# Pacing of expert tiles between attention turns: round length, a floor on the rest, and one exemption

## Chip, cores and metric

One core of one Trainium2 chip. The metric is the device time of one execution in microseconds (us); the kernel before takes 1529.41 us in the median of three executions (1528.07 to 1531.95).

## The reference

One transformer layer on x of shape (16, 512, 128), float32: attention with 16 heads of 8 and a residual, layernorm, then a mixture of 8 experts, of which each token uses two, a residual, layernorm.

```python
probs = softmax(Q @ K.T / sqrt(8)); iv = probs with key 0 set to 0, renormalised
x = layernorm(x + (0.5 * probs + 0.5 * iv) @ V @ Wo.T + bo)
wte = routing weights of the two chosen experts (0 for the other six)
out = sum over e of wte[:, e] * ((silu(x @ w1[e].T) * (x @ w3[e].T)) @ w2[e].T)
x = layernorm(x + out)
```

## The kernel before

**Turns.** The 16 sequences are worked on one after another, each in 32 turns (UNITS, line 998), 512 turns in all, numbered on from 0. A turn of attention (lines 1076 to 1088) has, on TensorE: two matmuls that spread the negated row maxima over a pair of PSUM banks (L451), two score matmuls for the maxima of 21 turns later (L399), two score matmuls (L456) and, in odd turns alone, the eight products of weights and values (L476). ScalarE takes the exponential of 128x1024 scores (L467). VectorE reduces 128x1024 scores to maxima (L405 to L408; the helper at L126 records it). In the trace a turn begins with its pair of L451 matmuls: there are 1024 of these rows, two for each turn.

**Small steps.** Everything else of the layer is written as generators which yield what they need (a bank: ONE, a pair: PAIR, a pause: REST, and so on). `everything()` (line 1055) hands out steps after each turn's attention. These small steps are projections, values, transposes after attention, routing, and the bank step of the maxima (`put_maxima`, line 410): four small transposes whose result goes by DMA to the tile `mt`, which the L451 matmuls of a later turn read.

**Rounds and tiles.** Tokens are scattered by expert into DRAM (L714, GpSimd) and worked on in tiles of 128 tokens of one expert, 149 tiles in all. Sequences form groups of 7, 7 and 2; each group has rounds, which become ready as attention moves on: of 9, 8, 8, 8, 8 and 22 tiles in a group of 7, and 23 in the last group. One tile takes 13 TensorE operations, called expert operations below: a transpose of the tokens (L133 with `xs`), eight matmuls up (L111 with `yx`, `ws`) and four down (L111 with `ws`, `hT`). Around them are a tanh (L858), a product on VectorE, a copy (L869), a product on GpSimd (L870), a copy of the down result and the transposed tokens to SBUF (L904), an indirect scatter (L912, GpSimd), and two loads that SyncE issues, of 64.5 KB of tokens (L824) and 768 KB of weights (L839). `down_and_turn` (line 877) takes one bank by `one()`: while experts run it is the single bank ELSE, shared with the small steps, and it comes free when ScalarE's copy at L904 has read it.

**The pace.** `experts(rnd)` (line 842) is a generator too. `running` holds the running rounds, two at most; only the first is advanced (line 1160), while the second merely issues its first loads. Work is counted in `dealt` by moving columns, two for each: 256 for an expert matmul, 128 for a transpose, 680 for an even attention turn and 1704 for an odd one. The pace of a turn is set at lines 1148 to 1176:

```python
goal = gen.left / max(gen.until - turn, 1)   # L1150, in the attention turns
goal += BASE                                 # L1155, BASE = 1450
carry += goal
while running and dealt[0] - before_turn < carry: ...one more step of running[0]...
carry = max(-600, min(1200, carry - dealt[0] + before_turn))
```

`left` is what the round still has to deal. `until` (line 1020) is the turn by which it should be through: the next round's earliest turn plus CHAIN (60) plus FILL (12). If the expert step asks for a bank and a small step has taken it in this turn, the expert step is put off and `owed` (line 1163) keeps small bank steps out of the next turn (lines 1116, 1117).

**After the last turn** the remaining tiles are worked on with no attention beside them (about 45 of the 149); here this is called the tail.

Of the kernel before, what the change touches and what calls it, by code (L numbers as in the profile page):

```python
# [33 lines left out]
def post_ln_layer(  # L34
# [375 lines left out]
    def put_maxima(b, half):  # L410

        yield NOW
        nm = nms.pop((b, half)).rearrange("p t s j -> p t j s")
        pc = small.tile([P, NT, 4, NPC, 2], BF16, tag="pc", name=f"pc{b}_{half}")
        for r in range(NPC):
            dve.tensor_copy(pc[:, :, :, r, :], nm)
            if r == 1:
                yield NOW
            if r < NPC - 1:
                rest = small.tile([P, NT, 4, 2], F32, tag="rest", name=f"rest{b}_{half}_{r}")  # L420
                dve.tensor_tensor(rest, nm, pc[:, :, :, r, :], ALU.subtract)
                nm = rest
        yield ONE
        n = 8 * NPC
        pm = one(BF16)
        for t in range(NT):
            turned(
                pm[0:n, t * P : (t + 1) * P],
                pc[:, t, :, :, :].rearrange("p j r s -> p (j r s)"), ident_b,
            )  # L430
        mT = work.tile([n, L], BF16, tag="mT", name=f"mT{b}_{half}", bufs=1)
        nc.scalar.copy(mT, pm[0:n, 0:L])
        mt = operands(b, half)[2]
        for j in range(4):
            nc.sync.dma_start(
                mt[HR * j : HR * j + NPC, :, :], mT[2 * NPC * j : 2 * NPC * (j + 1), :]
            )
# [565 lines left out]
    TOKENS = 4  # L1003
    PAUSE = 2400
    CHAIN = 60
    FILL = 12
    BASE = 1450
    TILE = 12 * 2 * P + P
    READY = [sum(GROUPS[:g]) + n for g, size in enumerate(GROUPS) for n in rounds_of(size)]
# [2 lines left out]
    class Steps:  # L1012
# [4 lines left out]
        def of(self, rnd):  # L1017
            self.rnd, self.left = rnd, rnd.tiles * TILE
            after = [n for n in READY if n > rnd.grp.first + rnd.n]
            self.until = UNITS * min(after, default=B) + CHAIN + FILL  # L1020
            return self
# [33 lines left out]
    def everything():  # L1055
        for gen in (project(0),):
            gen = Steps(gen)
# [4 lines left out]
        turn, last_final, carry, served = -LEAD, -UNITS, 0, dve.walked  # L1062
        before_turn, owed = dealt[0], False
        end = UNITS * B
        while turn < end + 2 or active or running or finishing or ready or late:
# [18 lines left out]
            if ahead:  # L1084
                reduce_maxima(*pm)
                if (turn + LEAD) % 16 == 15:
                    gen = put_maxima((turn + LEAD) // UNITS, (turn + LEAD) % UNITS // 16)
# [14 lines left out]
            if ready and all(gen.rnd.last for gen in running) and len(running) < 2:  # L1102
# [6 lines left out]
            gen = next((  # L1109
                gen for gen in active if gen.need == ONE  # L1110
                or gen.need == LONG and (not busy or gen.last is None or turn - gen.last > 1)
            ), None)

            if owed:
                gen = None
            taken = gen is not None and now
            order = [gen] if gen else []
# [27 lines left out]
                    gen.more()  # L1147
            if running:
                gen = running[0]
                goal = gen.left / max(gen.until - turn, 1)  # L1150
                if turn >= end:
                    goal = TILE // 2
                    spare[0] = 1 if gen.rnd.grp.g < len(GROUPS) - 1 or finishing else 0
                elif turn < end:
                    goal += BASE  # L1155
                carry += goal
            else:
                carry = 0
            while running and dealt[0] - before_turn < carry:
                gen, at = running[0], dealt[0]  # L1160
                if gen.need == TURN:
                    break
                owed = gen.need == ONE and taken
# [14 lines left out]
    with tc.manual_schedule(  # L1178
        engines={
            mybir.EngineType.PE, mybir.EngineType.DVE, mybir.EngineType.Activation,  # L1180
            mybir.EngineType.Pool, mybir.EngineType.SP,
        }
    ):
        everything()
# [37 lines left out]
```

## Time and profile before

| what | value |
|---|---|
| median of three executions | 1529.41 us |
| the profiled execution's own time, its span | 1559.23 us, 1557.5 us |
| turns 0 to 122, before the first expert operation | 49.3 to 338.4 us |
| turns 123 to 510 | 338.4 to 1359.5 us |
| last turn and tail | 1359.5 to 1557.5 us |
| L467 exponential, one | 1023 ns, x512 |
| maxima reduction on VectorE, one | 1220 ns, x512 |
| pair of passes of one expert matmul (L111), each pass | 285 ns, overlapping, x2384 and x1192 passes |

A row of the page's fifth part gives a group of instructions, its busy time, the mean of one in ns, and the idle time before it with what ended that. A float32 matmul has two passes on TensorE, so that its rows count double: four down matmuls are a row "x8". A window row gives, for a stretch of the span, its length, each engine's busy time with the number of instructions, and the granted TensorE clock as a share of full speed.

### The profile page before, as it was taken

How to read it: one execution, taken by the hardware profiler on the slowest of the kernel's cores; microseconds unless marked ns; L12 is line 12 of the kernel's file. 1: busy time of each engine (PE TensorE's matmuls, PEld its weight loads, DVE VectorE, ACT ScalarE, POOL GpSimd, SP SyncE). 2: the span in 40 equal slices, each digit the busy share in tenths (PEclk: the TensorE clock that was granted, in tenths of full speed). 3: DMA queues.
4: the chain of work that ended last, by engine and by line, in shares of the span. 5: the costliest groups of instructions: out<-in, count | busy, mean ns of one | idle time of the engine just before them, and what ended most of it. 6: DMA issues, size and time to landing. Idle time of an engine off the chain costs nothing.

```text
span 1557.5 us, 28295 instructions
## 1 busy us (share of the span) xinstructions
PE 1345.3 (86%) x9933; PEld 766.7 (49%) x9933; DVE 1062.4 (68%) x2221; ACT 890.8 (57%) x1383; POOL 674.6 (43%) x982
## 2 busy tenths in 40 slices
PE   4788888879889899999989999988898899997983
PEld 1222323225455555555555555555554555587883
DVE  5656576767876677767766776777777776465675
ACT  1355555555665666666656666666666677742333
POOL 2001031303534363626355463837364674756443
PEclk6577687868998999989999999999998999998996
DMA  5131443124443535363445366463633443576894
GB/s 187 50 92 65 130 126 118 56 83 172 164 138 129 196 131 193 115 212 129 136 172 173 143 209 209 140 214 110 216 127 104 172 161 126 204 246 230 304 344 155
DMA packets 114781, 248.43 MB, mean 160 GB/s; under 512 B 15232, under 2 KB 47104, under 8 KB 114640
## 3 DMA queue, kind: packets, MB, share of 16 engines
q1 hardware_dynamic: 95024, 220.01, 41.3%
q0 software_dynamic: 8864, 18.24, 3.4%
q10 hardware_dynamic: 10752, 8.39, 1.6%
q8 instruction: 78, 1.28, 0.3%
q14 instruction: 63, 0.52, 0.1%
HBM read 184.04 MB, written 68.04 MB: 162 GB/s over the span
## 4 chain that ended last, share of the span: by engine, by line
PE 56%; DVE 22%; ACT 10%; issue 5%; DMA 4%; POOL 2%; another core or an unknown queue 1%; SPq 1%; ACTq 0%; POOLq 0%; DVEq 0%
PE banks L111 23%; PE banks L476 14%; DVE nm L126 11%; PE banks L451 7%; PE banks L399 6%; ACT ex L467 6%; PE banks L133 4%; PE banks L456 2%; DVE lo L126 1%; ACT hi L339 1%; DMA z<-x1d 1%; DVE pc L126 1%; DVE th L126 1%; DVE z L126 1%
## 5 line engine op out<-in xcount | busy, mean ns | idle before, releaser
L126 DVE TENSOR_REDUCE nm<-banks 128x2 f32<-128x1024 f32 x512 | 623.4, 1220 | 320.9 <-PE banks L399 240.1
L467 ACT ACTIVATE ex<-banks 128x1024 f32<-128x1024 f32 x512 | 524.0, 1023 | 290.7 <-PE banks L456 241.1
L399 PE MATMUL banks<-kt,qt 32*128 32x512 f32 x1024 | 280.0, 548 | 78.6 <-DVE nm L126 57.8
L111 PE MATMUL banks<-yx,ws 128*128 128x128 f32 x2384 | 337.2, 285 | 7.2 <-DVE th L126 2.3
L111 PEld LDWEIGHTS banks<-yx,ws 128*128 128x128 f32 x2384 | 300.9, 197 | 63.3 <-issue 48.7
L476 PE MATMUL banks<-ex,vaug 128*32 128x512 f32 x2048 | 314.4, 690 | 0.0
L456 PE MATMUL banks<-qt,kt 32*128 32x512 f32 x1024 | 313.1, 605 | 0.0
L870 POOL TENSOR_TENSOR hT<-hT,th 128x512 f32<-128x512 f32 x104 | 132.6, 1275 | 337.7 <-ACT hT L869 249.8
L451 PE MATMUL banks<-mt,ones_b 3*128 3x512 bf16 x1024 | 216.3, 415 | 49.5 <-ACT ex L467 34.8
L912 POOL DMA_INDIRECT yd<-yx,toi x149 | 151.9, 1020 | 78.3 <-issue 35.3
L111 PE MATMUL banks<-ws,hT 128*128 128x128 f32 x1192 | 171.3, 289 | 4.3 <-ACT yx L904 2.7
L111 PEld LDWEIGHTS banks<-ws,hT 128*128 128x128 f32 x1192 | 157.3, 205 | 35.4 <-issue 27.6
L399 PEld LDWEIGHTS banks<-kt,qt 32*128 32x128 f32 x1024 | 103.0, 200 | 130.1 <-DVE nm L126 99.3
L451 PEld LDWEIGHTS <-ones_b 3*128 3x128 bf16 x1024 | 59.0, 93 | 193.4 <-issue 148.6
L714 POOL DMA_INDIRECT xg<-x,sloti x128 | 129.7, 1014 | 36.3 <-issue 25.9
L904 ACT COPY yx<-banks 128x128 f32<-128x128 f32 (+1 forms) x201 | 63.4, 316 | 131.5 <-PE banks L111 100.2
L858 ACT ACTIVATE th<-banks 128x512 f32<-128x512 f32 x149 | 88.9, 596 | 78.0 <-PE banks L111 56.2
L126 DVE SCALAR_TENSOR_TENSOR th<-th,banks 128x512 f32<-128x512 f32 x149 | 101.2, 679 | 46.4 <-ACT th L858 35.4
L456 PEld LDWEIGHTS banks<-qt,kt 32*128 32x128 f32 x1024 | 104.9, 201 | 0.0
L476 PEld LDWEIGHTS banks<-ex,vaug 128*32 128x32 f32 x2048 | 42.3, 113 | 88.0 <-issue 87.5
L509 POOL TENSOR_TENSOR both<-aw,den 128x256 f32<-128x256 f32 x60 | 37.9, 631 | 95.4 <-DVE den L126 95.4
L133 PE MATMUL banks<-ident,xs 128*128 128x128 f32 x149 | 47.8, 323 | 23.9 <-ACT yx L904 9.7
(161 smaller groups left out, 1274.8 us busy)
## 6 DMA issues: line engine op xcount, KB each, us to landing
ws<-wcat SPq DMA_DIRECT2D x149, 768.0 KB
qt<-qrow SPq DMA_DIRECT2D x32, 512.0 KB
kt<-krow SPq DMA_DIRECT2D x32, 512.0 KB
xs<-xg SPq DMA_DIRECT2D x149, 64.5 KB
qrow<-hi SPq DMA_DIRECT2D x32, 256.0 KB
qrow<-lo SPq DMA_DIRECT2D x32, 256.0 KB
krow<-hi SPq DMA_DIRECT2D x32, 256.0 KB
krow<-lo SPq DMA_DIRECT2D x32, 256.0 KB
```

The source lines that it names most:

```text
L111: nc.tensor.matmul(out, lhsT, rhs, start=start, stop=stop)
L126: return op(*args, **kwargs)
L133: nc.tensor.transpose(out, src, identity)
L399: nc.tensor.matmul(pm[:, u, :], qt[at, s, t * P : (t + 1) * P], kt[at, s, :], start=True, stop=True)
L451: nc.tensor.matmul(pc[:, u, :], ones_b[at : at + NPC, :], mt[at : at + NPC, g % 2, :], start=True, stop=False,)
L456: nc.tensor.matmul(pc[:, u, :], kt[at : at + HR, g % 2, c * P : (c + 1) * P], qt[at : at + HR, g % 2, :], start=False, stop=True,)
L467: nc.scalar.activation(ex, pair(ks), AF.Exp, scale=SCALE)
L476: nc.tensor.matmul(av[32 * j : 32 * j + 32, :], vas[b][:, c, 4 * g + j, :], ex[j // 2][:, j % 2, :], start=(c == 0), stop=(c == NT - 1),)
L714: put = nc.gpsimd.indirect_dma_start(out=grp.xg, out_offset=bass.IndirectOffsetOnAxis(ap=sloti[:, s, t : t + 1], axis=0), in_=x1[:, s, t, ...
L858: nc.scalar.activation(th, banks[:, ks[0], :], AF.Tanh, scale=0.5)
L870: nc.gpsimd.tensor_tensor(hT, hT, th, ALU.mult)
L912: put = nc.gpsimd.indirect_dma_start(out=grp.yd, out_offset=bass.IndirectOffsetOnAxis(ap=to, axis=0), in_=yx[:, 0, :], in_offset=None, bou ...
```

## The change

Three edits in the planner; no tile, operation or buffer differs.

```diff
-    FILL = 12
+    FILL = 6
+    SLOW = 8
...
-            if owed:
+            if owed and (gen is None or gen.gen.__name__ != "put_maxima"):
                 gen = None
...
-                goal = gen.left / max(gen.until - turn, 1)
+                goal = gen.left / max(gen.until - turn, SLOW)
```

FILL puts each round's `until` six turns earlier. SLOW divides the rest by eight turns at least, also when `until` is near or past. The third edit lets the bank step of the maxima through in a turn in which a bank is owed to the expert step.

The order of TensorE's instructions in the two built programs shows where the 13 operations of each tile fall. Expert operations in turns 224 to 255, one number for each turn:

```
before, 224-239: 4 2 2 6 2 4 0 6 4 0 0 7 2 5 4 5   240-255: 4 0 4 5 2 2 4 5 0 2 4 2 0 7 6 0
after,  224-239: 6 0 2 0 0 0 2 0 0 4 0 0 0 0 4 0   240-255: 13 2 0 14 6 7 4 0 11 0 11 2 6 0 0 8
```

Expert operations in stretches of 16 turns, from turn 192 on (the last stretch has 15, the last turn being counted with the tail):

```
from turn  192 208 224 240 256 272 288 304 320 336 352 368 384 400 416 432 448 464 480 496
before      57  51  53  47  57  51  66  67  76  69  65  56  57  51  55  49  53  53  64  54
after       36  66  18  84  26  80  18  89  96  79  44  75  20  84  26  78  42  70  49  67
```

From the last turn on, 593 expert operations are left before and 585 after.

## The prediction

> **What bounds the kernel now.** I read the page's busy shares first, then the chain, then windows, then one turn in the timeline.
>
> ```profile
> PE 1345.3 (86%) x9933; PEld 766.7 (49%) x9933; DVE 1062.4 (68%) x2221; ACT 890.8 (57%) x1383; POOL 674.6 (43%) x982
> ...
> PEclk6577687868998999989999999999998999998996
> ...
> PE 56%; DVE 22%; ACT 10%; issue 5%; DMA 4%; POOL 2%; another core or an unknown queue 1%; SPq 1%; ACTq 0%; POOLq 0%; DVEq 0%
> ```
>
> TensorE is the busiest engine and has over half of the chain that ended last, but not all of it: VectorE and ScalarE hold a third, because an attention turn passes back and forth between the three. The TensorE clock is low in the first fifth, where no expert tile exists, and nearly full afterwards. So expert work partly fills holes that attention leaves. The windows say how much (columns: stretch; length; busy us of PE, PEld, DVE, ACT, POOL with counts; granted clock; DMA share; GB/s). The first three rows are turns 64 to 79 (no expert operation), 256 to 271 (57) and 272 to 287 (51), the fourth 320 to 335 (76), the last the tail.
>
> ```profile
> 202.00:235.40 33.40, 28.29 (x200) 10.33 (x196) 24.85 (x37) 20.27 (x26) 15.45 (x26) 0.86 0.41 125
> 685.40:726.80 41.40, 39.21 (x313) 23.30 (x312) 29.86 (x63) 26.75 (x44) 19.96 (x27) 0.96 0.34 113
> 726.80:768.40 41.60, 38.17 (x296) 20.65 (x297) 33.10 (x70) 27.30 (x40) 17.32 (x20) 0.96 0.48 167
> 857.10:899.40 42.30, 39.96 (x339) 25.23 (x338) 32.71 (x57) 27.34 (x42) 21.77 (x35) 1.00 0.40 146
> 1359.50:1557.50 198.00, 149.16 (x1217) 139.98 (x1216) 118.55 (x375) 68.49 (x162) 98.58 (x136) 0.91 0.72 258
> ```
>
> Sixteen turns cost 33.4 us without experts and about 41.5 us with 50 to 57 operations, but 42.3 us with 76. The number of operations is therefore not the whole price; how they lie in the turns matters. The timeline of turn 263 shows a bad case, the end of a round:
>
> ```profile
> 702.90 0.39 PE L451 MATMUL banks<-mt,ones_b 3*128 3x512 bf16 x2 [0.59 <-ACT ex L467]
> ...
> 704.45 1.16 PE L111 MATMUL banks<-ws,hT 128*128 128x128 f32 x8
> 705.65 0.27 ACT L904 COPY yx<-banks 128x128 f32<-128x128 f32 x1 [1.00 <-PE banks L111]
> 706.06 1.13 PE L111 MATMUL banks<-ws,hT 128*128 128x128 f32 x8 [0.45 <-ACT yx L904]
> ...
> 707.54 0.33 PE L133 MATMUL banks<-ident,xs 128*128 128x128 f32 x1 [0.36 <-ACT yx L904]
> ...
> 708.23 0.33 PE L133 MATMUL banks<-ident,xs 128*128 128x128 f32 x1 [0.36 <-ACT yx L904]
> 708.39 0.61 PE L111 MATMUL banks<-yx,ws 128*128 128x128 f32 x4
> ...
> 708.94 0.39 PE L451 MATMUL banks<-mt,ones_b 3*128 3x512 bf16 x2
> ```
>
> At `until - turn` = 1 the whole rest is dealt at once: two down steps, then two token transposes, each waiting 0.36 to 0.45 us for the one shared bank. The next attention turn stands behind them: the turn takes 708.94 - 702.90 = 6.04 us.
>
> **The price of a turn.** For each of turns 123 to 510 I took its length from the trace (start of its first L451 matmul to the next turn's) and the number of expert operations in it from the program's order. Together they are 1021.1 us. Means by parity (odd turns carry L476) and number, and how many turns of each kind the order has before and after:
>
> ```
> operations        even: before, mean us, after   odd: before, mean us, after
> 0 to 3                  83    2.04       89            107    2.42      109
> 4 to 7                  92    2.39       70             71    3.29       63
> 8 to 11                 18    2.77       29             10    4.07       17
> 12 to 14: 7 turns before, 49.1 us together (6.04 to 8.82); 11 turns after
> ```
>
> **Part 1, SLOW and FILL: the round's end.** Six of the seven long turns (199, 263, 295, 359, 391, 423) are such round ends; they took 42.4 us together, and the order after has none of them. But a rest of at most 2048 now adds only 256 or less to BASE, so that attention's own mean of 1192 and the small steps use up most of the goal. Rounds end later, not sooner: at turn 238 instead of 231, 270 instead of 263, 363 instead of 359. Only the first running round is advanced, so that the next starts later as well, with an `until` six turns nearer: at turn 238 it has 25600 to deal in 20 turns (1280 a turn above BASE), where before it had 33 turns (776). The work goes into bursts of 11 to 14 operations, after some 14 nearly empty turns.
>
> **The sum.** Kinds below 12, change in number times mean: even 6 x 2.04 - 22 x 2.39 + 11 x 2.77 = -9.9; odd 2 x 2.42 - 8 x 3.29 + 7 x 4.07 = +7.0; together -2.9 us. The eleven long turns after: four (128, 240, 304, 400) open a round with two transposes, four up matmuls, a transpose and six more, exactly as turn 128 does before, which took 6.71 us: 26.8 us. The other seven have no such run of waits for the bank. I price them from the odd 8-to-11 kind (4.07 us at 8.7 operations) plus 4.9 operations at 0.275 us (in the 857 us window 46.5 up matmuls, L111 x93 passes, keep PE busy for 12.8 us): 5.4 us each, 37.8 us. So 64.6 us instead of 49.1: +15.5 us. Bounds: at 4.9 us each (two short stalls less) 53.9 us, +4.8; at the odd long turns' mean of 7.06 us, 77.7 us, +28.6. I take +15.5, as the opening turns have an exact row. The loop: +12.6 us (+1.9 to +25.7).
>
> What moves along with the matmuls: for each tile ScalarE's 596 + 585 + 316 ns, VectorE's 679 ns, GpSimd's 1275 and 1020 ns, and SyncE's loads of 64.5 and 768 KB. A dense half unit has about 6.5 tiles instead of 4: VectorE 33.1 + 1.7 us of some 45, GpSimd 17 + 6 us, DMA 2 MB more. The tail runs a tile in about 4 us at 258 GB/s, faster than the bursts, with a wait for `ws` of 1.2 us in all; so I cost these at nothing. If that cover went, one late load would stop the turn behind it for some microseconds, no more than a long turn above.
>
> **Part 2, the tail.** It holds 8 operations less: 8 x 0.275 = -2.2 us, at 0 if something else ends last there.
>
> **Part 3, the exemption.** The transposes of `put_maxima` stand in the same turns (12 and 28 of each 32) in both orders. What they guard costs next to nothing now:
>
> ```profile
> PEld L451 <- DMA mt<-mT: 2.4, 2, 1.9
> ...
> PE banks L451 <- DMA mt<-mT: 1.6, 2, 1.4
> ```
>
> So 0 us, at best -4. The sum is 12.6 - 2.2 = +10.4 us: 1559.2 to 1569.6 us for the profiled execution; in the ratio of the runs (1529.41 / 1559.23 = 0.981), **1539 us**, own range 1529 to 1553.
>
> **A rule that speaks against the change.** Row: turns 64 to 79, nearly empty of TensorE work but for attention, had a clock of 0.86 and still took only 33.4 us. The Trainium skill (TensorE: Matmul & The Clock Gate, the part on the HAM clock gate) says that TensorE falls to half rate after an idle window of about 3.4 us and needs as long a busy one to come back. By the rule each of the five new empty half units could lose the difference to the second half of that early unit (40.2 us at a clock of 0.71): up to 6.8 us each, +34 us. By the row, the same steps, it loses nothing beyond 33.4 us. I take the row: attention's pauses there are short. The opening burst can catch a low clock, which the 6.71 us of turn 128 contains.
>
> **Rivals.** (A) The empty half units pay for the bursts. In five units (halves from turn 224, 256, 288, 384, 416) the first half falls from 53 to 66 operations to 18 to 26. Before they took 37.5, 41.4, 44.4, 46.1 and 45.4 us, mean 43.0; at 33.4 us plus 21.6 x 0.14 (the slope between the first two window rows) 36.4: -33 us. The second halves (mean 42.8 us now) go to some 83 operations; at the 76-operation row plus 7 x 0.275 they take 44.2 us: +7. With the tail -28 us: 1502 us, clearly faster. It decides if dense halves stay under 42.8 + 6.6 = 49.4 us. For it: the fourth window row, and that TensorE has the attention of 16 turns done in 28 us. Against it: those 76 operations lie in turns of at most 11, and most of the projections and the transposes after layernorm lie in the second half too. If each of the 30 added operations cost its full 0.275 us, a dense half would take 51 us, and A would be lost. (B) Work is conserved and each operation costs the same wherever it lies: +8 operations in the loop, -8 in the tail, 1529 us. That the change does not do what it says is true of its third part already, and of rounds ending sooner; both are in the sum.
>
> **How the numbers follow.** This kernel's measurement tells 0.3%, some 4.6 us, from no change. The forecast, bursts dearer than the round ends they replace, has 0.60; B has 0.15; A has 0.25, between 1502 and 1524 us. So slower 0.60, same 0.15, faster 0.25. The range runs from 1514, in the middle of A, to 1556, above all long turns at 7.06 us; about 0.12 lies below it and 0.07 above.
>
> **What would show it.** Right: no 6 to 9 us turn at round ends; turns 240, 304 and 400 at over 6 us; second halves over 49.4 us, first halves near 36. Wrong: dense halves of 44 to 47 us (A), or a clock well below 0.86 in the empty halves, which would make it slower than forecast. A wait of L451 for `mt` over 4 us would mean that part 3 matters.

## The result and the profile after

The changed kernel takes 1594.33 us (median of four executions, 1589.71 to 1594.65), before 1530.54 us beside it: ratio 1.041, 95% interval 1.037 to 1.045. It is slower, by more than six times what was forecast (+64 us against +9.6), and above the range. Run again beside more executions of before (`after_again` below) the ratio is 1.030 (1.025 to 1.035). The level of before itself lies between 1531 and 1566 us from one set of runs to another, so only ratios within a set are compared below. The ratios leave out executions more than 1.5% longer than the fastest of the same kernel, so that they are not quite the quotients of the medians.

The page of the profiled execution after; its own time is 1589.71 us:

```profile
span 1587.8 us, 28310 instructions
...
PE 1363.1 (86%) x9933; PEld 783.4 (49%) x9933; DVE 1067.6 (67%) x2221; ACT 892.6 (56%) x1383; POOL 676.9 (43%) x982
...
PEclk7556777869999898999999999988999999989997
...
PE 53%; DVE 22%; ACT 11%; issue 5%; DMA 5%; POOL 3%; SPq 1%; ACTq 0%; POOLq 0%; DVEq 0%
```

The same 9933 matmul rows keep TensorE busy for 17.8 us longer than before, 1363.1 instead of 1345.3, at a mean granted clock of 0.881 instead of 0.897; the busy times of VectorE, ScalarE and GpSimd differ by 0.5% or less. The other part is idle time of TensorE, which grew from 212 to 225 us.

Windows of the changed kernel. First turns 0 to 122, then 123 to 510, then the last turn and the tail:

```profile
49.80:335.30 285.50, 244.33 (x1426) 80.92 (x1427) 185.99 (x288) 154.83 (x187) 45.06 (x75) 0.71 0.31 93
335.30:1394.50 1059.20, 946.75 (x7244) 551.97 (x7243) 728.91 (x1421) 665.65 (x1032) 528.75 (x757) 0.94 0.46 157
1394.50:1587.80 193.30, 149.18 (x1194) 141.01 (x1193) 120.19 (x375) 66.34 (x156) 94.01 (x131) 0.89 0.71 252
```

The same stages took 289.1, 1021.1 and 198.0 us in the profile before; its row for turns 123 to 510:

```profile
338.40:1359.50 1021.10, 929.84 (x7220) 536.77 (x7220) 725.32 (x1421) 661.70 (x1027) 522.01 (x751) 0.96 0.47 160
```

The whole loss is in turns 123 to 510: +38.1 us, of which 16.9 us are TensorE's busy time and 21.1 us its idle time. Some 2.2 us of the busy time are the eight operations that now lie here (an estimate, at 0.275 us each). The tail is 4.7 us shorter in this pair of traces. Next the half units of the forecast: turns 64 to 79 (no experts), 256 to 271 (26 operations), 272 to 287 (80), 384 to 399 (20), 400 to 415 (84):

```profile
204.70:240.20 35.50, 30.34 (x202) 11.28 (x198) 24.62 (x37) 20.27 (x26) 13.71 (x24) 0.78 0.33 100
685.40:726.80 41.40, 34.29 (x243) 16.37 (x243) 30.08 (x57) 22.35 (x33) 15.49 (x20) 0.88 0.29 99
726.80:775.50 48.70, 43.55 (x339) 27.17 (x338) 34.30 (x70) 29.63 (x45) 20.85 (x27) 0.96 0.48 162
1048.30:1091.50 43.20, 37.29 (x240) 17.33 (x239) 28.88 (x50) 23.29 (x35) 22.26 (x41) 0.76 0.37 133
1091.50:1142.80 51.30, 45.35 (x353) 28.38 (x352) 33.72 (x74) 33.23 (x55) 24.81 (x31) 0.97 0.60 198
```

Turns 256 to 271 take 41.4 us with 26 operations, exactly what they took with 57. TensorE's busy time fell by 4.9 us, and its idle time rose by as much, from 2.2 to 7.1 us. At 0.275 us each the 31 operations would have taken 8.5 us of busy time with them; the lower clock, 0.88 instead of 0.96 (0.76 in turns 384 to 399), goes with that shortfall. The dense half behind it pays 7.1 us for its 29 more operations. Over the five units with an empty half the first halves gave back 22 us for 180 operations less (0.12 us each), and the second halves took 28 us for 150 more (0.19 us each). These five units lose 6 us together. Most of the loss is in turns 320 to 383 (191.6 instead of 172.0 us, with 28 operations more) and 448 to 510 (168.1 instead of 152.9 us, with 4 more): TensorE is busy for 21.6 us longer there, with 37.8 instead of 3.4 us at half clock, and idle for 13.2 us longer.

Who kept TensorE waiting, from the waits of the changed kernel (us in total, times, longest):

```profile
PE banks L451 <- ACT ex L467: 50.2, 87, 2.7
...
PE banks L111 <- DVE th L126: 10.6, 14, 2.0
```

The same rows before:

```profile
PE banks L451 <- ACT ex L467: 34.8, 58, 1.7
...
PE banks L111 <- DVE th L126: 2.3, 3, 0.8
```

The first is the empty turn: nothing lies between one attention turn and the next, and the L451 matmuls wait until ScalarE's exponential has freed their banks. After turns without expert operations this wait is 45.3 us (76 times) instead of 26.3 us (43 times). The second is the burst. Turn 340, with 11 operations, in the timeline after:

```profile
916.65 0.39 PE L451 MATMUL banks<-mt,ones_b 3*128 3x512 bf16 x2
...
916.72 1.93 DVE L126 TENSOR_TENSOR pl_full<-rank,edges 128x224 f32<-128x224 f32 x1
...
918.26 1.06 PE L111 MATMUL banks<-yx,ws 128*128 128x128 f32 x8
...
919.41 1.21 DVE L126 TENSOR_REDUCE nm<-banks 128x2 f32<-128x1024 f32 x1
920.54 0.68 DVE L126 SCALAR_TENSOR_TENSOR th<-th,banks 128x512 f32<-128x512 f32 x1
...
921.27 0.71 PE L111 MATMUL banks<-yx,ws 128*128 128x128 f32 x4 [1.96 <-DVE th L126]
...
921.92 0.39 PE L451 MATMUL banks<-mt,ones_b 3*128 3x512 bf16 x2
```

Two tiles' up matmuls come in one turn, but there is one pair of banks for them. The second tile waits until VectorE has read the first one's bank for `th`, behind a reduction of maxima and a step of the planning of a round. TensorE stands still for 1.96 us and the turn takes 5.3 us. The two wait rows together grew by 23.7 us from before; some other waits became smaller.

### The profile page after: what moved, and what is told of

It is laid out like the page before. It is cut to its first block, busy times and chain, and to the rows that moved or that the text cites. A ratio compares the mean times of both kernels' runs of the same rounds, so it can differ in the third digit from the quotient of the medians.

```text
span 1587.8 us, 28310 instructions
## 1 busy us (share of the span) xinstructions
PE 1363.1 (86%) x9933; PEld 783.4 (49%) x9933; DVE 1067.6 (67%) x2221; ACT 892.6 (56%) x1383; POOL 676.9 (43%) x982
## 4 chain that ended last, share of the span: by engine, by line
PE 53%; DVE 22%; ACT 11%; issue 5%; DMA 5%; POOL 3%; SPq 1%; ACTq 0%; POOLq 0%; DVEq 0%
PE banks L111 21%; PE banks L476 13%; DVE nm L126 10%; PE banks L451 7%; ACT ex L467 6%; PE banks L399 6%; PE banks L133 4%; PE banks L456 2%; DMA yd<-yx,toi 2%; DVE th L126 1%; DVE z L126 1%; DVE lo L126 1%; ACT th L858 1%; ACT hi L339 1%; DMA z<-x1d 1%
## 5 line engine op out<-in xcount | busy, mean ns | idle before, releaser
L111 PE MATMUL banks<-yx,ws 128*128 128x128 f32 x2384 | 338.7, 288 | 16.8 <-DVE th L126 10.6
L399 PE MATMUL banks<-kt,qt 32*128 32x512 f32 x1024 | 284.2, 556 | 75.1 <-DVE nm L126 56.6
L111 PEld LDWEIGHTS banks<-yx,ws 128*128 128x128 f32 x2384 | 304.4, 200 | 66.5 <-issue 38.3
L456 PE MATMUL banks<-qt,kt 32*128 32x512 f32 x1024 | 319.7, 618 | 0.0
L476 PE MATMUL banks<-ex,vaug 128*32 128x512 f32 x2048 | 318.7, 699 | 0.0
L870 POOL TENSOR_TENSOR hT<-hT,th 128x512 f32<-128x512 f32 x104 | 132.3, 1272 | 338.4 <-ACT hT L869 267.8
L451 PE MATMUL banks<-mt,ones_b 3*128 3x512 bf16 x1024 | 219.6, 421 | 62.6 <-ACT ex L467 50.2
L912 POOL DMA_INDIRECT yd<-yx,toi x149 | 153.1, 1028 | 72.9 <-issue 25.1
L111 PE MATMUL banks<-ws,hT 128*128 128x128 f32 x1192 | 176.2, 295 | 4.5 <-ACT yx L904 2.1
L111 PEld LDWEIGHTS banks<-ws,hT 128*128 128x128 f32 x1192 | 160.2, 208 | 40.1 <-issue 20.5
L451 PEld LDWEIGHTS <-ones_b 3*128 3x128 bf16 x1024 | 61.1, 93 | 222.6 <-issue 182.3
L714 POOL DMA_INDIRECT xg<-x,sloti x128 | 129.8, 1014 | 39.7 <-issue 25.1
L869 ACT COPY hT<-banks 128x512 f32<-128x512 f32 x104 | 60.7, 583 | 16.4 <-PE banks L111 14.9
```

What stands on the lines that cost most here:

```text
L111: nc.tensor.matmul(out, lhsT, rhs, start=start, stop=stop)
L399: nc.tensor.matmul(pm[:, u, :], qt[at, s, t * P : (t + 1) * P], kt[at, s, :], start=True, stop=True)
L451: nc.tensor.matmul(pc[:, u, :], ones_b[at : at + NPC, :], mt[at : at + NPC, g % 2, :], start=True, stop=False,)
L456: nc.tensor.matmul(pc[:, u, :], kt[at : at + HR, g % 2, c * P : (c + 1) * P], qt[at : at + HR, g % 2, :], start=False, stop=True,)
L476: nc.tensor.matmul(av[32 * j : 32 * j + 32, :], vas[b][:, c, 4 * g + j, :], ex[j // 2][:, j % 2, :], start=(c == 0), stop=(c == NT - 1),)
L714: put = nc.gpsimd.indirect_dma_start(out=grp.xg, out_offset=bass.IndirectOffsetOnAxis(ap=sloti[:, s, t : t + 1], axis=0), in_=x1[:, s, t, ...
```

## The experiments

Theories: U, uneven spreading over the turns (bursts, B, and empty turns, E); F, the shorter time for a round (FILL) as such; C, the TensorE clock; and single stalls that each new order happens to make. "Half-clock time" is the time for which the trace's clock records show half rate, within turns 123 to 510: 88.7 us before, 136.8 us after. "Idle" is TensorE's, in the same turns: 91.3 us before, 112.4 us after.

**exempt_only**: the third edit alone (FILL 12, no floor).

> The exemption of the maxima's bank step alone (FILL 12, no floor). Its order of instructions on every engine is that of the kernel before, so every theory expects no change: ratio 1.000 within 0.3%. It also shows how far a profiled execution of this program lies from its timed ones (1559 against 1529 us so far).

Ratio 0.997 (0.993 to 1.001): nothing, as the equal order of TensorE's instructions says. Its profile shows what an execution of the program of before can also look like, by the same three stages:

```profile
49.30:308.50 259.20, 213.51 (x1426) 73.43 (x1427) 185.75 (x288) 154.26 (x187) 45.06 (x75) 0.85 0.34 102
308.50:1323.00 1014.50, 927.52 (x7220) 537.69 (x7220) 725.79 (x1421) 662.96 (x1027) 523.55 (x751) 0.96 0.47 161
1323.00:1516.60 193.60, 150.29 (x1217) 142.26 (x1216) 118.66 (x375) 68.61 (x162) 98.77 (x136) 0.90 0.74 263
```

Turns 0 to 122 took 30 us less than in the profile on which the forecast was made, at a clock of 0.85 instead of 0.72, with the same instructions. So a comparison of two whole spans can be off by 30 us. Turns 123 to 510 differ by 7 us here; with two more traces of the same order there (`before_early_warm` and `before_early_one` below) they take 1012.4 to 1030.6 us. A difference of less than some 20 us between single traces of this stage therefore shows nothing.

**fill6_only**: `FILL = 12` -> `FILL = 6`, no floor.

> FILL 6 alone, no floor. The order has 100 turns without expert operations (104 before, 145 in the changed kernel) and half units of 39 to 80 operations, as before. Theory U (the loss comes from uneven spreading: empty turns and dense half units): within 1% of before, 1520 to 1545 us. Theory F (the loss comes from having less time for a round): a good part of the loss, over 1555 us.

Ratio 1.019 (1.013 to 1.025), turns 123 to 510 1038.8 us: U's forecast for it failed, since its half units are as even as before, and the 1555.81 us are, just, what F expected. Its waits have a row that before has with 0.9 us, "PE banks L111 <- POOL hT L870: 18.8, 9, 3.8". A round end in its timeline, turn 255 and 256:

```profile
669.57 0.39 PE L451 MATMUL banks<-mt,ones_b 3*128 3x512 bf16 x2
...
671.21 0.58 ACT L869 COPY hT<-banks 128x512 f32<-128x512 f32 x1
671.88 1.27 POOL L870 TENSOR_TENSOR hT<-hT,th 128x512 f32<-128x512 f32 x1 [2.48 <-ACT hT L869]
...
673.20 1.16 PE L111 MATMUL banks<-ws,hT 128*128 128x128 f32 x8 [3.01 <-POOL hT L870]
```

The last tiles of a round are finished so close together that the down matmuls come up before GpSimd's product is done, and TensorE waits 3.01 us.

**slow8_only**: `max(gen.until - turn, 1)` -> `max(gen.until - turn, 8)`, FILL 12.

> The floor of eight turns alone, FILL 12. 112 turns without expert operations, half units of 30 to 47 and 66 to 80 operations by turns, one turn of 12 or more. Theory U: about half of the loss of 4.1%, 1550 to 1575 us. Theory F: near before, 1525 to 1540 us. Theory C (the loss is the low TensorE clock of nearly empty half units): a loss only if the granted clock of the sparse halves falls below 0.93.

Ratio 1.012 (1.007 to 1.018), between the theories: about a third of the loss. Half-clock time is 75.1 us, so C does not explain it, but idle is 109.2 us. In turn 304 of its timeline:

```profile
779.71 0.97 POOL L912 DMA_INDIRECT yd<-yx,toi  x1 [0.31 <-issue]
781.00 0.97 POOL L714 DMA_INDIRECT xg<-x,sloti  x1 [0.32 <-issue]
782.28 0.98 POOL L912 DMA_INDIRECT yd<-yx,toi  x1 [0.30 <-issue]
783.56 0.97 POOL L912 DMA_INDIRECT yd<-yx,toi  x1 [0.30 <-issue]
785.65 0.27 ACT L904 COPY yx<-banks 128x128 f32<-128x128 f32 x1 [8.47 <-DMA yd<-yx,toi]
...
785.97 0.47 PE L133 MATMUL banks<-ident,xs 128*128 128x128 f32 x1 [6.77 <-ACT yx L904]
```

The old round ends later, and its result scatters (L912) stand among scatters of tokens (L714) on GpSimd's queue. The next round's first copy needs one of the four `yx` buffers, waits for such a scatter to land, and TensorE stands 6.77 us. Such a stall comes twice more (3.2 us in turn 368, 7.0 us in turn 464). That these stalls are the loss is not shown: more `yx` buffers, which would test it, were not tried.

**slow3**: FILL 12, a floor of three turns.

> FILL 12 and a floor of three turns in place of eight. 97 turns without expert operations, half units as even as before, and only one turn of 12 or more in place of seven. If the round-end turns of 6 to 9 us cost what the prediction said (some 3 us each over an ordinary turn), this saves 10 to 20 us: 1510 to 1520 us. If they only do early what must be done anyway, within 0.3% of before.

Ratio 1.007 (1.004 to 1.010): a miss. The long round-end turns of before are gone (one of seven left) and nothing is won; it is rather a little slower. So those turns were no loss that this floor could save.

**after_again**: the changed kernel once more.

> The changed kernel once more, beside more runs of before, since executions of one program spread by 1% (1512 to 1547 us for before). All theories: 1580 to 1600 us. What the profile adds: turns 123 to 510 at about 1059 us against 1015 to 1021 before, whatever turns 0 to 122 take in that execution.

1601.08 us beside 1556.81: ratio 1.030 (1.025 to 1.035). Turns 123 to 510 take 1063.2 us, half-clock time is 122.9 us, idle 123.1 us, and the two waits are 51.1 and 10.3 us: the loss sits where it sat, also with a short first stage (269.1 us). Beside exempt_only the stage is 48.7 us longer, which agrees with this set's ratio.

**after_warm**: the changed kernel with idle matmuls in the empty turns.

```diff
+            dealt_till = dealt[0]
...
+            if 123 <= turn < end - 1 and dealt[0] == dealt_till:
+                k = max(sorted(freed), key=age)
+                for _ in range(2 - n % 2):
+                    nc.tensor.matmul(banks[:, k, 0:P], ident, ident, start=True, stop=True)
```

> The changed kernel plus idle work: in each of the 145 turns from 123 on that deals no expert operation, two (even turns) or one (odd turns) 128x128 float32 matmuls of the identity into a free bank that nobody reads, 206 in all, some 57 us of TensorE if they were not in its pauses. Theory C (low clock in the empty turns and at the start of the bursts behind them is a good part of the loss): time at half clock in turns 123 to 510 falls from 137 us to under 95 and the kernel gets faster, 1565 to 1585 us. Theory U without C (bursts and unused pauses alone): half-clock time matters little, the time stays or grows, 1590 to 1630 us.

Ratio 1.033 (1.026 to 1.039): no gain. Idle falls from 123.1 to 84.9 us and half-clock time stays at 120.9 us, while turns 123 to 510 grow to 1078.2 us. The clock rises in the five empty halves (0.91 to 1.00 there, instead of 0.76 to 1.00), but these get only 1.2 us shorter on average, the dense halves behind them 1.4 us longer, and TensorE's busy time grows by 53 us in the stage. So filling these pauses is no remedy. As half-clock time did not fall, the run does not show what the low clock itself costs.

**both_rounds_paced**: the changed kernel, pace over both running rounds.

```diff
-                goal = gen.left / max(gen.until - turn, SLOW)
+                goal = sum(g.left / max(g.until - turn, SLOW) for g in running)
```

> The changed kernel with the goal summed over both running rounds instead of the first alone, so that a rest of one round no longer holds back the next: 116 empty turns instead of 145, half units of 41 to 74 operations instead of 18 to 96, FILL 6 and the floor kept. Theory U: most of the loss goes, 1535 to 1555 us (fill6_only with as few empty turns took 1556). If instead the floor as such costs (down steps in turns where they hold up small steps): over 1575 us.

Ratio 1.031 (1.026 to 1.036), a miss: half units are even again and nothing is won. Idle is 124.9 us, now with 17.9 us of waits for GpSimd's hT. So empty half units alone are not the cause, and removing them brought the stall of fill6_only, which the changed kernel does not have (no wait for GpSimd's hT in its trace).

**fill6_quick**: fill6_only, with the last two products of a round on VectorE.

```diff
-                if tail[0]:
-                    dve.tensor_tensor(hT, th, banks[:, ks[1], :], ALU.mult)
+                if tail[0] or k >= K - 2:
+                    (dve if tail[0] else nc.vector).tensor_tensor(hT, th, banks[:, ks[1], :], ALU.mult)
```

> FILL 6 alone, and the products hT of a round's last two tiles made by VectorE from the bank, as in the tail, instead of a copy by ScalarE and a product on GpSimd; order of TensorE as in fill6_only. There TensorE waited 18.8 us for hT from GpSimd at round ends (0.9 us in before), in turns 160, 256, 352, 384, 416, 480 and 508. If these waits, and the half-clock stretches behind them, are the cause of fill6_only's 1.9%, the waits fall under 4 us and the ratio to before is 0.998 to 1.008. If the loss lies elsewhere, the ratio stays at 1.015 or more.

Ratio 1.002 (0.998 to 1.006) against 1.019: as expected for the single stall. The waits for GpSimd's hT are gone from its trace. Its one profiled execution, a long one of 1583.83 us beside the median of 1568.02, does not show the gain in the stage: 1038.2 us with 107.7 us idle, since other waits grew there (L451 for the exponential from 17.5 to 28.4 us). So the times of many executions carry this verdict, not the trace. With FILL still 6, it also speaks against F. What these products would do in the kernel before was not run; its waits for hT are 0.9 us.

**after_cap6**: the changed kernel, no expert step started in an attention turn once 1280 columns are dealt to experts.

```diff
-            while running and dealt[0] - before_turn < carry:
+            till = dealt[0]
...
+            while running and dealt[0] - before_turn < carry and (turn >= end or dealt[0] - till < 1280):
```

> The changed kernel with a cap: in an attention turn no further expert step is started once 1280 columns (five matmuls) have been dealt to experts in it. The sparse and dense half units stay (24 to 50 and 65 to 80 operations by turns, 128 empty turns), but of 57 turns with 8 to 14 operations one is left. Theory B (bursts within a turn are dear: even turns of 8 to 11 cost 3.38 us instead of 2.77, VectorE's release of the pair is waited for): 30 us of the loss go, ratio to before 1.005 to 1.015, TensorE's waits for th under 4 us. Theory E (the empty turns, in which TensorE waits for the exponential and its clock drops): ratio 1.02 or more, waits of L451 for ex still 45 us or more, half-clock time in turns 123 to 510 above 110 us.

Ratio 1.014 (1.008 to 1.020), B's upper end, in place of 1.030 to 1.041: the cap takes off half of the loss or more. It is not bursts alone that it removes, since 128 empty turns are left instead of 145. And its profiled execution, one of the longer ones (1600.74 us beside the median of 1593.86), shows no shorter stage: 1060.0 us, with waits for `th` of 5.6 us (B expected under 4), for the exponential of 56.6 us and 150.2 us at half clock, all that E expected. Taken alone the run leaves open how the loss divides.

**both_quick**: both_rounds_paced with the VectorE products of fill6_quick.

> both_rounds_paced (1.031, half units even) with the hT products of a round's last two tiles made by VectorE, so that the 17.9 us of TensorE's waits for GpSimd's hT go; order of TensorE unchanged. If stalls at single places are the loss: 1.010 to 1.020, in proportion to fill6_quick, which lost 1.7 points. If the loss comes from the floor or the bursts: 1.025 or more.

Ratio 1.016 (1.013 to 1.019) in place of 1.031: half of this version's loss went with the waits for one product, as expected.

**both_quick_cap**: the same with the cap of after_cap6.

> The same with the cap of 1280 columns of expert work for each turn: no waits for GpSimd's hT, no empty half units (34 to 75 operations), 14 turns of 8 or more instead of 39, 108 empty turns. Theories B and E together (bursts and empty half units make the loss, besides single stalls): level with before, 0.995 to 1.008, though FILL 6 and the floor are still in. If it stays over 1.015, something of FILL or the floor that I have not named costs.

Ratio 0.999 (0.995 to 1.002): level with before, with FILL 6 and the floor still in. Turns 123 to 510 of the three versions, first both_rounds_paced:

```profile
336.70:1402.40 1065.70, 940.80 (x7235) 544.55 (x7235) 721.64 (x1424) 660.56 (x1027) 532.03 (x767) 0.94 0.45 154
```

both_quick:

```profile
315.80:1359.80 1044.00, 938.42 (x7232) 541.68 (x7232) 730.22 (x1446) 652.35 (x1005) 500.03 (x744) 0.94 0.46 156
```

both_quick_cap:

```profile
325.10:1342.80 1017.70, 927.96 (x7240) 533.22 (x7239) 732.44 (x1442) 655.75 (x1009) 498.13 (x736) 0.95 0.47 160
```

Here trace and times agree: 1065.7, 1044.0, 1017.7 us for the same tiles. Idle goes 124.9, 105.6, 89.7 us; half-clock time 133.1, 126.3, 99.0 us. F has fallen: the shorter time for a round costs nothing measurable once empty half units, bursts and the wait for one product are gone together.

**before_cap**: the kernel before with the cap.

> The kernel before with the cap alone: no turn of 12 or more operations instead of 7, 10 of 8 to 11 instead of 28, 93 empty turns instead of 104, tail and half units as before. Theory B: 0.985 to 0.997. If the long turns of before only do early what must be done anyway (slow3, with one long turn, gave 1.0065): 0.998 to 1.008.

Ratio 1.000 (0.997 to 1.003). The few bursts of before cost nothing that the cap could save; like slow3 it speaks against the prediction's reading of turn 263 as a loss.

**before_early_warm, before_early_one, before_cap_early**: an idle matmul or two in turns 0 to 122, where no expert tile exists, in before or in before_cap. The edit of before_early_warm; the other two have one matmul in each turn:

```diff
+            dealt_till = dealt[0]
...
+            if 0 <= turn < 123 and dealt[0] == dealt_till:
+                k = max(sorted(freed), key=age)
+                for _ in range(2 - n % 2):
+                    nc.tensor.matmul(banks[:, k, 0:P], ident, ident, start=True, stop=True)
```

> The kernel before plus the same idle matmuls in those turns 0 to 122 in which no expert operation is dealt (all of them), 185 in all. Theory C: the first stage, 259 to 289 us long with 79 to 160 us at half clock, gets to about 250 us with less than 50 us at half clock, and the kernel to 1500 to 1520 us with less spread. Without C: no change or up to 50 us slower.

> The kernel before with one idle matmul in each of turns 0 to 122 (123 in all) instead of two in even turns and one in odd (185, ratio 0.989). Theory C: the clock needs only few more busy microseconds; the first stage is at most 20 us shorter or longer than with 185, ratio 0.980 to 0.992. If one is too few to keep the clock up, over 50 us at half clock in the first stage and a ratio near 0.995 to 1.000.

> before_cap with one idle matmul in each of turns 0 to 122. If the two effects add, before_cap's ratio less 0.010 to 0.014; the best of these versions if before_cap is not slower than before.

Ratios 0.989 (0.985 to 0.993), 0.986 (0.979 to 0.993) and 0.986 (0.980 to 0.993). Turns 0 to 122 of before_early_warm:

```profile
50.80:313.30 262.50, 244.45 (x1796) 116.93 (x1797) 185.71 (x288) 153.95 (x187) 44.97 (x75) 0.97 0.34 101
```

More matmuls (1796 rows instead of 1426), a clock of 0.97, and 262.5 us. The other 14 traces have one and the same order of TensorE's instructions in these turns: they take 259.2 to 297.9 us (277.5 us on average), at a clock of 0.68 to 0.85, with 79 to 191 us at half clock. The three with idle matmuls take 262.1 to 263.8 us, with 17 to 45 us at half clock. These versions beat both kernels by over 1%; the gain lies in turns that the change does not touch, and the cap adds nothing to it.

## Why the prediction was wrong

**The direction** (slower, 0.60) was right, the size was not: +64 us in the times, +38.1 us in turns 123 to 510 of the traces, where +12.6 was forecast. The forecast owed its direction to the long turns, at +15.5 us; they measured +6.3 us, a sixth of the loss. So the direction was in good part luck. Of its signs of being right, no long round end came, but only one of turns 240, 304 and 400 took over 6 us, and the dense halves stayed under 49.4 us.

**The step that failed** is "Kinds below 12, change in number times mean: together -2.9 us". It took the mean of a kind of turn from before as its price after, so that the turns that it took for ordinary came out at nothing. Measured, these kinds changed by +31.7 us: even turns +10.7 (forecast -9.9), odd ones +21.0 (forecast +7.0). Even turns of 8 to 11 operations cost 3.38 us instead of 2.77 (29 turns, 17.7 us more than priced). They hold 9.8 operations instead of 8.8 on average, some 8 us (an estimate, at 0.275 us each): the table put both into one kind. And TensorE was idle for 0.7 us in the 18 turns before and is for 9.1 us in the 29 now, 5.6 us of it waiting for `th`. Odd turns of 0 to 3 cost 2.55 instead of 2.42 us (109 turns, 14.2 us more than priced): TensorE's idle time in them grew from 12.6 to 26.2 us, mostly in waits for the exponential (9.2 to 13.1 us) and for VectorE's reduction of maxima (1.9 to 9.3 us), and half-clock time from 18.9 to 37.2 us. The same kind of turn had another price in the new order, and a table of the old one could not say so.

**The long turns** were priced too high, not too low: 64.6 us forecast, 55.3 us measured (60.4 us in after_again). The four opening turns took 6.82, 5.29, 6.09 and 5.29 us, not 6.71 each. Turn 128 before, the row for them, ran at half clock for 6.2 of its 6.71 us; after, the two slower ones have 6.1 and 3.3 us of that, the other two none. The other seven took 4.5 us on average, not 5.4.

**The rule that was weighed** (the Trainium skill, TensorE: Matmul & The Clock Gate, on the HAM clock gate) was put aside for the row of 33.4 us. That was half wrong. The five empty halves took 38.5 us on average, not 36.4, at clocks of 0.86, 0.88, 1.00, 0.76 and 0.91. They did not lose the 6.8 us each that the rule allowed, but the lower clock is there: in turns 123 to 510 half-clock time went from 88.7 to 136.8 us and TensorE's busy time up by 16.9 us. The page asks for an idle window before a fall; in these traces a window that was half busy was enough (last section).

**Cover for what moves along.** "I cost these at nothing" was wrong for one queue: in slow8_only the moved scatters stand among others on GpSimd and a 6.77 us stall comes of it. In the changed kernel itself TensorE's transposes wait little for the copies of `yx` (9.1 us, 8.6 in exempt_only), so this does not carry its loss.

**Rival A** missed too: dense halves took 48.5 us on average, under the 49.4 that were to decide for it, and the kernel was still slower: its 36.4 and 44.2 us were both too low, and it left out turns 320 to 383 and 448 to 510, where 35 us of the loss are. **Part 2** cannot be judged: the tail took 193.3 and 198.7 us in two traces of the changed kernel, 198.0 and 193.6 us in two of the order before. **Part 3** was right: the `mt` rows are 2.4 and 1.6 us again, and exempt_only gains nothing. **Scaling** a sum by 0.981 rested on a profiled execution whose first stage was 30 us longer than another one of the same program; the profiled before was 29 us over the median beside the changed kernel, the profiled after 5 us under its own.

**What stays open.** The additions speak for one picture: FILL alone 1.9 and the floor alone 1.2 points, together 3.0 to 4.1; with the cap 1.4 left in the changed kernel; without bursts, empty halves and the product's wait nothing left. That last wait came in only with the even pace of both_rounds_paced; the changed kernel has none of it. How the changed kernel's loss divides between bursts and empty turns is not settled, since the cap changes both and after_cap6's trace did not shorten with its times. What its lower clock costs by itself is open too, and why the first set gave 4.1% and the second 3.0%.

## What to carry to other kernels

Where several engines pass work back and forth, the mean price of a step in the old order is no price for a new order: new neighbours make new waits for single buffers, so look for each reused resource (a bank pair, a ring of four, an in-order queue) at what the new order puts in front of it. A smoother end of one job that holds back the next only moves the crowding, and even spacing pays only when the last producer before each consumer is quick enough. Compare traces stage by stage, and know how far a stage differs between executions with the same instructions: here by up to 39 us in a stage that the change does not touch, and by up to 18 us in the one it does.

## What the runs showed of the hardware

TensorE's clock goes with its own business, in steps of about 3.4 us: all of its records in the traces of before and after but the last are whole multiples of that. In the trace of before, cut into such windows from 330 us on, 22 windows at full clock were followed by half clock: TensorE was busy for 0.56 of them in the median. In the 300 followed by full clock it was 0.97, though 0.52 in the lowest, so no threshold can be read from this. The 21 returns to full clock each came after a window that was busy throughout (after: 31 falls, median 0.54; 30 returns, after windows busy for 0.90 or more). From 50 to 330 us, where only attention and small steps run, 35 windows at half clock were busy for 0.96 in the median and were followed by half clock again; all 10 returns came after windows busy throughout.

What a step at half clock costs can be estimated from pairs of traces. From exempt_only to the changed kernel, 51.5 us more at half clock go with 19.2 us more of TensorE's busy time, 2.2 of them for eight operations more: 0.33 us for each. From exempt_only to before_early_warm, the same order in these turns, 27.3 us less go with 11.0 us less: 0.40. By that a step of 3.4 us costs 1.1 to 1.4 us. A window busy for 0.56 has a pause of 1.5 us, so that such a stall can cost nearly as much again behind it. And in a stage with little work, 123 matmuls that nobody reads made the kernel 1.4% faster.
